# Delta rule in units of two heads: second unit's queries in the score banks, fifth unit's keys in the first chunk, a half's layer norm in the middle of the unit behind

## The chip, the cores and the metric

The kernel runs on one core of a Trainium2 chip. The metric is the device time of one execution in microseconds, the median over timed runs. The engines are PE (TensorE, with its weight loads as PEld), DVE (VectorE), ACT (ScalarE), POOL (GpSimd) and SP, which here only issues DMA transfers.

## The reference

Two transformer layers with post layer norm, on x of 2 batches x 1024 tokens x 256:

```python
def layernorm(x): m = mean(x); v = var(x); return (x - m) / sqrt(v + 1e-5)

x = layernorm(x + L0_attn(x))   # softmax attention, 32 query heads of 8, 8 key/value heads, rotary, causal
x = layernorm(x + L0_ffn(x))    # down(silu(x @ gate * s_gate) * (x @ up * s_up)) * s_down, int8 weights, 256 -> 1024 -> 256
x = layernorm(x + L1_attn(x))   # below
x = layernorm(x + L1_ffn(x))    # sign weights, relu, 256 -> 1024 -> 256

# L1_attn, 16 heads of 128
q, k, v = [silu(causal_depthwise_conv4(x @ W) + b) for W, b in (q, k, v)]
alpha, beta = sigmoid(x @ Wa + ba), sigmoid(x @ Wb + bb)
for t in range(T):              # S: 128 x 128 for each head
    err = S @ (k[t] * scale) - v[t]
    S = alpha[t] * S - beta[t] * outer(err, k[t] * scale)
    o[t] = S @ q[t]
o = (o - mean(o)) * rsqrt(var(o) + 1e-5) * ln_w + ln_b
return (o * sigmoid(x @ Wg)) @ Wo
```

## The kernel before

The kernel has three stretches. Up to about 679 us it does the first layer's attention and half of its int8 feed-forward. From there the second layer's attention begins beside the rest of the feed-forward, which ends with PE's last down product at 802.5 us. The delta rule proper fills the time to about 1950 us, and the second feed-forward runs in its last units and behind it.

The delta rule is worked in 32 **units**: a half of 512 tokens (there are four, `hi`) times a pair of heads (eight pairs, `s`; unit i is `hi, s = divmod(i, 8)`). A unit is four chunks of 128 tokens. `recur` goes through the chunks one after the other: `pr` (values turned, minus decayed keys times the state M), `prs` its copy on ACT, `pw` (times the inverse of the triangle `lt`), `wc` its copy, `pm` (the state's update, taken up by DVE into the next M, L697 or L699) and `po` (the outputs `o`).

Everything else of the neighbour units stands in between by **places**. A unit has 120 places. Each stream of work (`Places.add`) is a generator that yields the place at which it goes on; `Places.run` always takes the stream with the lowest place, and for the same place the one added first. From unit 0 on PE's order is exactly the order in which this emits the products (`te.strict`); the other engines' orders are made by the framework's scheduler, which simulates the program and prefers what was emitted earlier or marked `high_priority`. `after(a, b)` orders a behind b on their engine.

The parts that matter here:

- `project`, `conv`, `conv_out`: the queries, keys or values of a unit. Two banks (one for each head) take 6 products each; ACT scales a bank into `acc` (L268) and keeps its last three columns in `halos` (L272), DVE adds two taps of the convolution (L275), ACT makes the third (`far`, L289), POOL adds it (L292), ACT applies silu (L297). All projections take their banks from one pool of two, `ps_p` ("p"). The pool `ps_m` ("m", two banks) is for scores, turned keys, the gates and others.
- `keys`: the keys of unit i + 4 at place 91, then their triangle at 113 to 146: scans along the tokens (`at`, L325) and the products `pkk`.
- `rest_of_first`: emitted between the feed-forward's last block and unit 0. It loads the decays `dg` of unit 0, multiplies its keys and queries by them on POOL (L519, L521), then projects unit 1's values and queries, then unit 4's keys.
- `blocks` and `levels`: the triangle's inverse for two units, in chains of small DVE steps (L384, L390) and small products with copies (L420 to L479).
- `finish`: a unit's outputs, in the unit behind it, at places 41, 51, 101 and 111. The head outputs are normed (bias L595, scale on DVE, ACT and POOL, L602 and L605), turned (`pt`, L611), gated, split for precision (POOL, L618) and multiplied by Wo into `pf`; DVE adds that to the tokens `x` (L630). The pool of `x` (`xtok`) has one buffer, loaded for a half at its first unit's `finish`. At the half's last unit (`s == 7`) `finish` norms the tokens, two tiles after each `pf`, and stores them to `xs`, from where the second feed-forward takes them.
- `layernorm` (L919): for each tile of 128 tokens `bn_stats` and `bn_aggr`, then `rsqrt` over both tiles: three DVE steps (L905 to L907) and three rounds, either on DVE (three steps each, L910 to L912) or on POOL (four steps each, L914 to L917), then a DVE scaling for each tile (L926). The int8 feed-forward's blocks take POOL for the rounds; `finish` takes DVE.

The tokens `x` of the int8 feed-forward lie where the pools "late" and "w" are opened later, so the first tiles of these (`prs`, `dg`, `wg`) come after the last store of `x`.

The lists of places:

```python
UNIT, GAP = 120, 10
AT_ROWS, AT_QUERIES, AT_KC, AT_GATE, AT_GATE_ROWS, AT_SCORES = 1, 31, (42, 52), 61, 70.5, (71, 81)
AT_OUT = 9.5
AT_KEYS, AT_DECAY, AT_TRIANGLE = 91, 113, (131, 141, 146)
AT_LEVELS = 43, 53, 73, 83, 103, 113, 132, 142
AT_FINISH, AT_FINISH_LAST, AT_HALF = (41, 51, 101, 111), (31, 41, 71, 76), ((22, 30, 46), (12, 18, 36))
```

Of the kernel before, what the change touches and what calls it, by code (L numbers as in the profile page):

```python
# [31 lines left out]
HP = 2  # L32
# [56 lines left out]
AT_LEVELS = 43, 53, 73, 83, 103, 113, 132, 142  # L89
AT_FFN = 24  # L90
AT_FINISH, AT_FINISH_LAST, AT_HALF = (41, 51, 101, 111), (31, 41, 71, 76), ((22, 30, 46), (12, 18, 36))
# [53 lines left out]
def delta_rule(  # L145
# [39 lines left out]
    def bank(pool, tag, name):  # L185
        return pool.tile([P, HT], F32, name=name, tag=tag)
# [51 lines left out]

    def project(m, i, h):
        hi, s = place(i)  # L240
        if h == 0 and ("w" + m) not in st[i]:
            st[i]["w" + m] = weights(m, s)
        wh, wl = st[i]["w" + m]
        xh, xl = halves[hi]["xh"], halves[hi]["xl"]
        pp = bank(ps_p, "p", "pp")
        hs = slice(h * P, (h + 1) * P)
        for k in range(2):
            mm3(pp, wh[:, k, hs], wl[:, k, hs], xh[:, k, :], xl[:, k, :], k == 0, k == 1)
        return pp
# [10 lines left out]
    def conv(m, i, h, pp):  # L260
# [6 lines left out]
        with tc.high_priority():  # L267
            nc.scalar.activation(  # L268
                acc, pp, AF.Identity, bias=cb[:, n, hd : hd + 1], scale=cw[:, n, hd, KS - 1 : KS]
            )  # L270
            if hi % 2 == 0:
                nc.scalar.copy(halos[:, n, hd, :], pp[:, HT - KS + 1 :])  # L272

            for d in range(1, KS - 1):
                made = nc.vector.scalar_tensor_tensor(  # L275
                    acc[:, d:], pp[:, 0 : HT - d], cw[:, n, hd, KS - 1 - d : KS - d], acc[:, d:], ALU.mult, ALU.add
                )
                if m == "k" and d == 1 and solved:
                    after(made, solved[-1])
# [200 lines left out]

    def pair(m, i):

        pps = [project(m, i, h) for h in range(HP)]
        for h in range(HP):
# [73 lines left out]
    def rest_of_first():  # L558
# [4 lines left out]
        te.strict, te.last = True, ended[0]  # L563
        for m in "vq":
            drain(pair(m, 1))
        ks = keys(AHEAD, AT_KEYS)
        next(ks)
        lines.add(ks, next(ks), 0)

# [5 lines left out]
    def finish(i, o, m, chunks, places):  # L575

        hi, s = place(i)
        if s == 0:
            halves[hi]["x"] = load_tokens(pools["late"], hi * HC, HC)
        x = halves[hi]["x"]  # L580
        if chunks[0] == 0:
# [25 lines left out]
        for h in range(HP):  # L607
# [11 lines left out]
            sub_low(nc.gpsimd if i < last else nc.vector, yl, y, yh)  # L619
            ys.append((yh, yl))  # L620
        for c0 in range(0, nc_, 2):
            yield places[2 + c0 // 2]
# [7 lines left out]
            nc.vector.tensor_add(xc, pf, xc)  # L630
            if s == NS - 1:
                layernorm(gx, x, c1 + c0, 2)
                halves[hi]["done"] = c1 + c0 + 2
        if s == NS - 1 and hi < 2 * B - 1:
            store_tokens(xs, hi * HC, x)
# [183 lines left out]
    for i in range(-AHEAD, last + 1):  # L819
# [19 lines left out]
        elif 0 <= i < last:  # L839
            lines.add(others(i + 1), t + AT_ROWS, t)  # L840
        if i == 0:
            lines.add(gate_of_first(), t + AT_QUERIES)
        if i >= 0:
# [28 lines left out]
def tile_two_layers(ctx: ExitStack, tc: tile.TileContext, a, out):  # L872
# [45 lines left out]

    def layernorm(pool, x, t0, n, tag="ln", eng=None):  # L919
        m = pool.tile([P, n, 11], F32, name=tag, tag=tag)  # L920
        for i in range(n):
            nc.vector.bn_stats(m[:, i, 5:11], x[:, t0 + i, :])
            nc.vector.bn_aggr(m[:, i, 0:2], m[:, i, 5:11])
# [535 lines left out]
    def open_ffn(group):  # L1459
# [20 lines left out]
        def block(n):  # L1480
# [45 lines left out]
            with tc.high_priority() if n == NT - 2 else nullcontext():  # L1526
                for i in range(2):
                    y = new("fy", [P, E], 2)
                    nc.vector.tensor_mul(y, po[i], s_down)
                    nc.vector.tensor_add(x[:, n + i, :], y, x[:, n + i, :])  # L1530
                anchor["norm"] = layernorm(pool, x, n, 2, eng=nc.gpsimd)
                store_tokens(xs, n, x[:, n : n + 2, :])
# [129 lines left out]
```

## Time and profile before

| | us |
|---|---|
| timed runs | 2059.25, 2059.91, 2062.58 (median 2059.91) |
| the profiled execution | 2060.95 |
| its span in the trace | 2059.2 |
| mean granted PE clock | 0.979 |
| DVE, ACT, POOL busy | 1481.1, 1268.1, 1055.6 |
| last product of the int8 feed-forward | 802.5 |
| first `prs` copy of unit 0, of unit 1 | 819.8, 846.6 |
| end of the last layer norm of the int8 feed-forward; issue of its store | 814.7; 814.70 |
| issues of the stores of a finished half's tokens | 1148.4, 1742.0 (first and last of three) |

How to read it. One execution was taken; times count from its first instruction. PE's busy time is modelled from the start of each product, so a busy PE need not be at its peak. In a time line each row has a start, a length, the engine, the line, what is written and read, and in brackets how long the engine had been idle and which instruction released it. A wait for several things is put down to the one that came last. A granted clock of 1.00 is full speed; at 0.50 a product of 512 columns starts 0.43 us after the one before it instead of 0.23.

### The profile page before, as it was taken

Reading aid. Unit: us, or ns where it says so; the run is one execution under the profiler, and the core shown is the slowest. Engines: PE = TensorE matmul, PEld = TensorE weight load, DVE = VectorE, ACT = ScalarE, POOL = GpSimd, SP = SyncE. Lnnn points to the kernel's source line nnn. Section 1 sums busy time; section 2 is a strip of 40 time slices with the busy share of each in tenths; the row PEclk is TensorE's granted clock in tenths of the full one; section 3 lists DMA queues with packets and bytes.
Section 4 is the critical chain, followed back from the end, with each engine's and each line's share of the span. In section 5 each row is a group of like instructions: output and inputs, shape, how many; then the busy total and the mean of one; then the engine's idle time right before and its main releaser. Section 6 shows DMA issues by size and latency. Waiting matters only on the chain.

```text
span 2059.2 us, 49201 instructions
## 1 busy us (share of the span) xinstructions
PE 1891.8 (92%) x18657; PEld 1493.3 (73%) x18657; DVE 1481.1 (72%) x3557; ACT 1268.1 (62%) x2731; POOL 1055.6 (51%) x1635
## 2 busy tenths in 40 slices
PE   5898989999998898999999999998999999999886
PEld 3455555555556786889888888887888888888775
DVE  5756666877756886586778688678678678865676
ACT  1365566576755366567676676766677666686432
POOL 4353332331124565666776566666567676665430
PEclk8999999999999999999999999999999999999997
DMA  5554443442132432344444444444434434442010
GB/s 169 167 188 131 149 130 126 147 135 70 51 76 62 116 91 82 111 132 106 132 110 115 133 109 116 115 118 123 123 109 125 124 115 130 118 126 86 26 37 21
DMA packets 312997, 229.16 MB, mean 111 GB/s; under 512 B 139640, under 2 KB 278904, under 8 KB 312760
## 3 DMA queue, kind: packets, MB, share of 16 engines
q1 hardware_dynamic: 299640, 210.73, 35.1%
q10 hardware_dynamic: 9760, 10.83, 1.6%
q0 software_dynamic: 3360, 4.46, 0.9%
q8 instruction: 147, 2.41, 0.5%
q14 instruction: 90, 0.74, 0.1%
HBM read 171.18 MB, written 51.87 MB: 108 GB/s over the span
## 4 chain that ended last, share of the span: by engine, by line
PE 57%; DVE 13%; ACT 6%; DMA 5%; POOL 3%; issue 3%; SPq 1%; ACTq 0%; DVEq 0%; POOLq 0%
PE pp L942 5%; PE pp L944 4%; PE pp L943 4%; PE ps L1316 4%; PE av L1337 4%; PE ps L1247 3%; PE pkq L508 3%; PE pm L692 2%; DVE at L325 2%; PE pr L669 2%; PE pw L680 2%; PE po L708 2%; PE po L707 2%; PE p L478 2%; PE p L471 2%
## 5 line engine op out<-in xcount | busy, mean ns | idle before, releaser
L1256 DVE TENSOR_REDUCE mx<-ps 128x4 f32<-128x1024 f32 (+1 forms) x320 | 344.1, 1111 | 131.8 <-PE ps L1247 88.5
L1320 ACT ACTIVATE es<-ps 128x512 f32<-128x512 f32 (+1 forms) x608 | 314.2, 578 | 128.8 <-PE ps L1316 118.1
L1316 PE MATMUL ps<-qT,kT 128*128 128x512 f32 (+3 forms) x768 | 220.8, 371 | 19.4 <-ACT es L1320 18.6
L1247 PE MATMUL ps<-kT,qT 128*128 128x512 f32 x576 | 199.2, 420 | 26.8 <-DVE mx L1256 16.9
L1316 PEld LDWEIGHTS ps<-qT,kT 128*128 128x128 f32 x768 | 130.9, 190 | 106.4 <-ACT es L1320 59.6
L1247 PEld LDWEIGHTS ps<-kT,qT 128*128 128x128 f32 x576 | 101.6, 191 | 86.5 <-DVE mx L1256 45.8
L289 ACT ACTIVATE far<-pp,cw 128x509 f32<-128x509 f32 x192 | 133.4, 700 | 45.5 <-DVE k L275 18.6
L1337 PE MATMUL av<-es,vaug 128*32 128x512 f32 (+3 forms) x1536 | 157.7, 497 | 0.6 <-POOL es L1323 0.5
L1323 POOL TENSOR_SCALAR_AFFINE_SELECT es<-es 128x512 f32<-128x512 f32 x128 | 80.5, 638 | 147.0 <-ACT es L1320 144.0
L891 POOL TENSOR_TENSOR wfl<-wf,wfh 128x256 fp32r<-128x256 f32 x80 | 58.5, 735 | 185.7 <-ACT wfh L980 147.3
L275 DVE SCALAR_TENSOR_TENSOR q<-pp,cw,q 128x511 f32<-128x511 f32 (+1 forms) x128 | 93.3, 743 | 46.5 <-ACT halos L272 23.8
L275 DVE SCALAR_TENSOR_TENSOR k<-pp,cw,k 128x511 f32<-128x511 f32 (+1 forms) x128 | 92.1, 743 | 46.5 <-ACT k L268 25.3
L292 POOL TENSOR_TENSOR q<-q,far 128x509 f32<-128x509 f32 x64 | 69.5, 1088 | 95.0 <-ACT far L289 94.9
L275 DVE SCALAR_TENSOR_TENSOR v<-pp,cw,v 128x511 f32<-128x511 f32 (+1 forms) x128 | 92.2, 739 | 32.4 <-ACT v L268 18.2
L292 POOL TENSOR_TENSOR k<-k,far 128x509 f32<-128x509 f32 x64 | 77.8, 1217 | 52.0 <-ACT far L289 51.4
L519 POOL TENSOR_TENSOR k<-k,dg 128x508 f32<-128x508 f32 x64 | 82.2, 1284 | 33.7 <-PE pkq L508 29.8
L980 ACT CAST wfh<-wf 128x256 fp32r<-128x256 f32 x80 | 32.3, 405 | 105.9 <-DMA wf<-in_w1k 35.5
L708 PE MATMUL po<-wc,at 128*128 128x128 f32 x512 | 96.8, 276 | 0.0
L672 ACT COPY prs<-pr 128x256 f32<-128x256 f32 x128 | 48.9, 382 | 73.9 <-PE pr L669 65.8
L325 DVE TENSOR_TENSOR_SCAN at<-da,d 128x512 f32<-128x512 f32 x64 | 90.4, 1453 | 0.0
L680 PEld LDWEIGHTS pw<-prs,lt 128*128 128x128 f32 x512 | 76.7, 191 | 15.9 <-ACT prs L672 3.2
L692 PE MATMUL pm<-wc,kc 128*128 128x128 f32 x448 | 77.2, 295 | 11.8 <-ACT wc L683 11.7
(319 smaller groups left out, 5902.6 us busy)
## 6 DMA issues: line engine op xcount, KB each, us to landing
wk<-w1k SPq DMA_DIRECT2D x64, 256.0 KB
da<-dec SPq DMA_DIRECT2D x64, 256.0 KB
wv<-w1v SPq DMA_DIRECT2D x64, 256.0 KB
wq<-w1q SPq DMA_DIRECT2D x64, 256.0 KB
dg<-dec SPq DMA_DIRECT2D x64, 256.0 KB
wg<-w1g SPq DMA_DIRECT2D x64, 256.0 KB
wo<-w1o SPq DMA_DIRECT2D x64, 256.0 KB
ad<-avs ACTq DMA_DIRECT2D x32, 256.0 KB
```

The source lines that it names most:

```text
L275: made = nc.vector.scalar_tensor_tensor(acc[:, d:], pp[:, 0 : HT - d], cw[:, n, hd, KS - 1 - d : KS - d], acc[:, d:], ALU.mult, ALU.add)
L289: made = nc.scalar.activation(far[:, w], pp[:, w], AF.Copy, scale=cw[:, n, hd, 0:1])
L292: nc.gpsimd.tensor_add(acc[:, KS - 1 :], acc[:, KS - 1 :], far[:, w])
L325: nc.vector.tensor_tensor_scan(e, dec, d1.rearrange("p c t -> p (c t)"), 0.0, ALU.mult, ALU.add), taps
L680: te.link(nc.tensor.matmul(pw[:, r], lhsT=lt[:, h * HC + c, :], rhs=prs[:, r], start=True, stop=True))
L692: te.link(nc.tensor.matmul(pm[:, r], lhsT=st[i]["kc", h][:, c, :], rhs=wc[:, r], start=True, stop=True))
L708: te.link(nc.tensor.matmul(po[:, r], lhsT=st[i]["at", h][:, t], rhs=wc[:, r], start=(M is None), stop=True))
L1247: anchor["mm"] = te.link(nc.tensor.matmul(ps[:, j - j0, :].rearrange("p (g k) -> p g k", k=P), lhsT=q_, rhs=kT[:, :, j * P : (j + 1) * P], ...
L1256: nc.vector.tensor_reduce(mx[:, it, j0 // 2, :], ps[:, 0:n, :].rearrange("p j (g k) -> p g j k", k=P), AX.XY, ALU.max)
L1316: te.link(nc.tensor.matmul(ps[:, g - g0, :], lhsT=kT[:, g, jb * P : (jb + 1) * P], rhs=qT[:, i0 : i0 + w], start=True, stop=True,))
L1320: exps.append(nc.scalar.activation(es[:, g0 : g0 + n, 0:w], ps, AF.Exp, scale=D ** -0.5))
L1337: mm = te.link(nc.tensor.matmul(av[ROW * g : ROW * (g + 1), i0 - ih * 512 : 512], lhsT=vaugs[b][:, jb, kv, :], rhs=es[:, g, 0:w], start=(j ...
```

## The change

It has five parts.

1. `project` takes a pool as an argument, and `rest_of_first` gives the pool "m" to unit 1's queries. Values stay in "p".
2. Unit 1's value taps (`conv`, the first tap of `v` at `i == 1`) are ordered behind the last layer norm of the int8 feed-forward (`anchor["norm"]`). The rounds of that last block's `rsqrt` go to DVE; the other blocks keep POOL.
3. Unit 4's keys leave `rest_of_first`. They become a stream of unit 0, `first_keys`: projection and taps at place 1, the third tap and silu at 10.5, the rest at 113 and on as before.
4. A finished half's layer norm and store (all halves but the last) leave the places 101 and 111 of the unit behind its last unit and go to places 34 and 50 of the unit after that one (units 9, 17, 25), two tiles at each. The statistics are ordered behind the newest update of M that is emitted by then, and the `rsqrt` rounds run on POOL. The last half keeps its norm where it was.
5. The load of a half's tokens moves within `finish` from its start to just before place 101.

```diff
--- before.py
+++ after.py
@@ -87,7 +87,7 @@
 AT_KEYS, AT_DECAY, AT_TRIANGLE = 91, 113, (131, 141, 146)
 AT_BLOCKS, BLOCK_STEP = (44, 52, 145), 2.2
 AT_LEVELS = 43, 53, 73, 83, 103, 113, 132, 142
-AT_FFN = 24
+AT_FFN, AT_NORM = 24, (34, 50)
 AT_FINISH, AT_FINISH_LAST, AT_HALF = (41, 51, 101, 111), (31, 41, 71, 76), ((22, 30, 46), (12, 18, 36))
 
 FFN0, FFN1, FFN1_LAST, FFN1_TAIL = 7.6, 22.0, 27.0, 40.0
@@ -236,13 +236,13 @@
 
         return divmod(i, NS)
 
-    def project(m, i, h):
+    def project(m, i, h, psum=None):
         hi, s = place(i)
         if h == 0 and ("w" + m) not in st[i]:
             st[i]["w" + m] = weights(m, s)
         wh, wl = st[i]["w" + m]
         xh, xl = halves[hi]["xh"], halves[hi]["xl"]
-        pp = bank(ps_p, "p", "pp")
+        pp = bank(*(psum or (ps_p, "p")), "pp")
         hs = slice(h * P, (h + 1) * P)
         for k in range(2):
             mm3(pp, wh[:, k, hs], wl[:, k, hs], xh[:, k, :], xl[:, k, :], k == 0, k == 1)
@@ -275,6 +275,8 @@
                 made = nc.vector.scalar_tensor_tensor(
                     acc[:, d:], pp[:, 0 : HT - d], cw[:, n, hd, KS - 1 - d : KS - d], acc[:, d:], ALU.mult, ALU.add
                 )
+                if m == "v" and i == 1 and d == 1:
+                    after(made, anchor["norm"])
                 if m == "k" and d == 1 and solved:
                     after(made, solved[-1])
         return made
@@ -478,9 +480,9 @@
                     te.link(nc.tensor.matmul(p4[A, u, :], lhsT=n3[Z, u, :], rhs=lt[Z, u, Z], start=True, stop=True))
             nc.scalar.copy(st[i + n]["lt"][A, :, Z], p4[A])
 
-    def pair(m, i):
-
-        pps = [project(m, i, h) for h in range(HP)]
+    def pair(m, i, psum=None):
+
+        pps = [project(m, i, h, psum) for h in range(HP)]
         for h in range(HP):
             conv(m, i, h, pps[h])
         if i < last:
@@ -561,11 +563,16 @@
             for h in range(HP):
                 decayed(0, h, which)
         te.strict, te.last = True, ended[0]
-        for m in "vq":
-            drain(pair(m, 1))
+        for m, psum in (("v", (ps_p, "p")), ("q", (ps_m, "m"))):
+            drain(pair(m, 1, psum))
+
+    def first_keys():
+
         ks = keys(AHEAD, AT_KEYS)
         next(ks)
-        lines.add(ks, next(ks), 0)
+        yield AT_ROWS + AT_OUT
+        yield next(ks)
+        yield from ks
 
     def gate_of_first():
         gate(0)
@@ -575,9 +582,6 @@
     def finish(i, o, m, chunks, places):
 
         hi, s = place(i)
-        if s == 0:
-            halves[hi]["x"] = load_tokens(pools["late"], hi * HC, HC)
-        x = halves[hi]["x"]
         if chunks[0] == 0:
             st[i]["wo"] = []
             for part in range(2):
@@ -618,6 +622,9 @@
             (nc.gpsimd.tensor_copy if i < last else nc.scalar.copy)(yh, y)
             sub_low(nc.gpsimd if i < last else nc.vector, yl, y, yh)
             ys.append((yh, yl))
+        if s == 0:
+            halves[hi]["x"] = load_tokens(pools["late"], hi * HC, HC)
+        x = halves[hi]["x"]
         for c0 in range(0, nc_, 2):
             yield places[2 + c0 // 2]
             pf = bank(pools["t"], "t", "pf").rearrange("p (c e) -> p c e", e=E)
@@ -628,10 +635,15 @@
                     mm3(pf[:, c, :], yh[:, t], yl[:, t], wo[0][:, h, :], wo[1][:, h, :], h == 0, h == HP - 1)
             xc = x[:, c1 + c0 : c1 + c0 + 2, :]
             nc.vector.tensor_add(xc, pf, xc)
-            if s == NS - 1:
+            if s == NS - 1 and i == last:
                 layernorm(gx, x, c1 + c0, 2)
                 halves[hi]["done"] = c1 + c0 + 2
-        if s == NS - 1 and hi < 2 * B - 1:
+        if s == NS - 1 and i < last:
+
+            for n in range(0, HC, 2):
+                yield UNIT + AT_NORM[n // 2]
+                made = updated[-1]
+                layernorm(gx, x, n, 2, eng=nc.gpsimd, behind=made)
             store_tokens(xs, hi * HC, x)
 
     def recur(i):
@@ -839,6 +851,7 @@
         elif 0 <= i < last:
             lines.add(others(i + 1), t + AT_ROWS, t)
         if i == 0:
+            lines.add(first_keys(), t + AT_ROWS, t)
             lines.add(gate_of_first(), t + AT_QUERIES)
         if i >= 0:
             lines.add(recur(i), t, chain=True)
@@ -916,10 +929,12 @@
                 eng.tensor_scalar(t, t, -0.5, 1.5, ALU.mult, ALU.add)
                 eng.tensor_mul(y, y, t)
 
-    def layernorm(pool, x, t0, n, tag="ln", eng=None):
+    def layernorm(pool, x, t0, n, tag="ln", eng=None, behind=None):
         m = pool.tile([P, n, 11], F32, name=tag, tag=tag)
         for i in range(n):
-            nc.vector.bn_stats(m[:, i, 5:11], x[:, t0 + i, :])
+            made = nc.vector.bn_stats(m[:, i, 5:11], x[:, t0 + i, :])
+            if behind:
+                after(made, behind)
             nc.vector.bn_aggr(m[:, i, 0:2], m[:, i, 5:11])
         rsqrt(m[:, :, 2], m[:, :, 1], m[:, :, 3], m[:, :, 4], eng=eng)
         for i in range(n):
@@ -1528,7 +1543,7 @@
                     y = new("fy", [P, E], 2)
                     nc.vector.tensor_mul(y, po[i], s_down)
                     nc.vector.tensor_add(x[:, n + i, :], y, x[:, n + i, :])
-                anchor["norm"] = layernorm(pool, x, n, 2, eng=nc.gpsimd)
+                anchor["norm"] = layernorm(pool, x, n, 2, eng=nc.gpsimd if n < NT - 2 else None)
                 store_tokens(xs, n, x[:, n : n + 2, :])
             yield 0.2
```

## The prediction

> **What bounds it now.** I read the page's busy table first, then the matrix engine's idle stretches, then the units one by one, then the queues behind the two worst places. The profiled execution took 2060.95 us, of which the trace spans 2059.2 us. The median of the three timed runs, 2059.91 us, is 1.04 us lower.
>
> ```profile
> PE 1891.8 (92%) x18657; PEld 1493.3 (73%) x18657; DVE 1481.1 (72%) x3557; ACT 1268.1 (62%) x2731; POOL 1055.6 (51%) x1635
> ```
>
> PE is busy 92% of the span, so what can be won lies in the 167 us in which PE waits, and in the stretches where its clock is halved. I took the start of a unit from its first `prs` copy on ACT (L672) and asked for the busy time between such starts. Columns: length, then busy us of PE, PEld, DVE, ACT, POOL, granted clock, DMA share, GB/s. These are units 7, 9, 15, 17, 23 and 25, and last the seam from the last product of the int8 feed-forward to the start of unit 1:
>
> ```profile
> 1055.50:1095.30 39.80, 37.92 (x654) 33.61 (x653) 29.38 (x76) 28.15 (x60) 28.66 (x48) 1.00 0.40 115
> 1128.90:1172.40 43.50, 37.88 (x646) 33.67 (x645) 32.08 (x104) 27.49 (x61) 25.19 (x41) 0.96 0.43 128
> 1351.30:1390.50 39.20, 37.05 (x650) 33.06 (x650) 26.81 (x62) 27.09 (x65) 26.76 (x41) 1.00 0.40 113
> 1421.30:1471.20 49.90, 40.11 (x651) 34.77 (x651) 35.43 (x105) 28.94 (x67) 27.00 (x41) 0.90 0.39 114
> 1649.00:1688.80 39.80, 37.75 (x654) 33.62 (x653) 29.42 (x76) 28.02 (x60) 28.62 (x48) 1.00 0.40 116
> 1722.40:1761.90 39.50, 36.58 (x648) 32.50 (x647) 32.08 (x104) 27.30 (x60) 25.68 (x42) 1.00 0.46 142
> 802.50:846.60 44.10, 33.71 (x170) 27.30 (x169) 27.11 (x79) 20.84 (x50) 22.24 (x31) 0.85 0.49 152
> ```
>
> Units 9, 17 and 25 have about 28 more DVE instructions than 7 and 23: the layer norm of a finished half falls at their start. It costs 10.1 us in unit 17 (49.9 against 39.8), 3.7 us in unit 9 and nothing in unit 25. How, the time lines of PE and DVE in unit 17 show (start, length, engine, instruction, idle time before it and its releaser):
>
> ```profile
> 1441.06 1.07 PE L611 MATMUL pt<-ident,o 128*128 128x128 f32 x3 [7.11 <-POOL o L605]
> ...
> 1439.99 0.79 DVE L926 TENSOR_SCALAR xtok<-xtok,ln 128x256 f32<-128x256 f32 x2
> 1440.70 0.16 DVE L595 SCALAR_TENSOR_TENSOR om<-om 128x8 f32<-128x8 f32 x1
> ```
>
> L595 makes the bias for the head outputs. It stands in DVE's queue behind the last rows of the norm, so `o` is scaled late and PE's transposes L611 wait 7.11 us; PE runs the next 5 us (1441 to 1446) at a granted clock of 0.50. The seam, on PE and DVE:
>
> ```profile
> 807.29 0.50 PE L942 MATMUL pp<-x2h,wq 128*128 128x512 f32 x1 [1.81 <-ACT far L289]
> 813.41 0.50 PE L942 MATMUL pp<-x2h,wk 128*128 128x512 f32 x1 [1.51 <-ACT far L289]
> 816.59 0.49 PE L942 MATMUL pp<-x2h,wk 128*128 128x512 f32 x1 [1.51 <-ACT far L289]
> 820.24 0.68 PE L680 MATMUL pw<-prs,lt 128*128 128x128 f32 x4 [1.77 <-issue]
> 826.03 0.77 PE L669 MATMUL pr<-M,k 128*128 128x128 f32 x2 [1.81 <-DVE M L697]
> ...
> 813.62 1.04 DVE L926 TENSOR_SCALAR x<-x,ln 128x256 f32<-128x256 f32 x1
> 814.67 0.73 DVE L275 SCALAR_TENSOR_TENSOR q<-pp,cw,q 128x510 f32<-128x510 f32 x1
> ```
>
> Each projection waits until ACT's `far` has read the bank it wants; the last layer norm ends at 814.66, and its store, the `dg` and `wg` loads and the first tile of the late pool queue behind it. PE does 33.7 us of work in 44.1 us, 10 of them at half clock (821.6 to 831.9).
>
> **The seam, step by step.** Unit 1's values stay at 802.5 to 805.5. Its queries now take the two `m` banks, last read at 797.2 by L1042, so they follow at once: 12 products at 0.235 us, to 808.3. The norm reaches its aggregates at 804.9 as before. Then, instead of 12 POOL steps among `v` adds (808.36 to 812.60), DVE does 12 dependent steps 0.20 us apart (the pace of the last norm in the program, 2031.07 to 2033.07): 2.4 us, and two scalings, 0.7 us, so 808.0, or 809.5 if two query taps of 0.75 us get between. I take 808.5 in place of 814.66. New wait: the value taps (4 x 0.75 us) stand behind it, 808.5 to 811.5; behind them in DVE's queue are the query taps and the solve of units 2 and 3, and who waits is ACT's `far`, so the `p` banks. The first bank is free at 810.9 (tap, 0.2, `far` 0.69), the second at 812.4. Unit 4's keys, now after unit 0's first transposes, are 6 products each, 811.0 to 812.4 and 812.5 to 813.9; PE loses 2.3 us ahead of them. The store goes out at 808.6 (wq's two loads, 811.70 and 812.15 before, stand ahead of it on SP and wait for the same queries, 808.3), lands 2.1 us later (814.70 to 816.84), so `prs` is ready at 811. `pw` follows the keys at 814.0, for 820.24.
>
> The next wait is `pr` of the second chunk (826.03), which needs M and the decayed keys. M: `pm` would end at 816, M at 816.5; with the two scans of unit 4 ahead of it in DVE's queue, as now (821.36 to 825.58), up to 3 us more. Decayed keys: the first L519 started at 819.87, 4.7 us after the first `dg` issue at 815.16; that issue moves to 809.1, so 813.8, then three POOL products at 1.27 us, and one or two of the six 1.09 us adds between: 818.7. I take 818.7: 7.3 us earlier. Of the half clock after 821.6 (some 6 us of work in 825 to 832, 3 us at full clock) I count 1 us back, since a gap of 2.3 us stays. Seam: -8.3. Bounds: -2, if the queries' and keys' ACT and POOL work, now crowded into a shorter stretch, leaves only the 1.8 and 1.5 us waits; -12, if M is not behind the scans and all the clock comes back. The moved keys bring nothing new: 12 products, 4 taps, 8 ACT instructions, 2 POOL adds and two `wk` loads for unit 5, out of the stretch before unit 0 into it, under unit 0's own waits.
>
> The Trainium skill speaks against the last microsecond: TensorE: Matmul & The Clock Gate, section "What's actually happening", has the clock drop after an idle window of about 3.4 us. The trace has a clock of 0.51 in 825 to 832 though no idle stretch of the seam is over 1.81 us. By the page the clock gives 0 here and the seam -7.3.
>
> **The half's norm.** It leaves the start of units 9, 17, 25 for their places 34 and 50 of 120, behind the first chunk's M. Gone: 10.1 us in unit 17; in unit 9 1.3 us surely (the level product L431 waits 2.26 us there and 0.7 to 1.2 elsewhere), 3.7 at most, since 1.65 us of its idle time is put down to issue: 2.5; in unit 25 0. New: per unit 4 statistics (0.41), 4 aggregates (0.17), 6 small steps (0.16) and 4 scalings (0.41), 4.9 us of DVE, less 18 steps (2.9 us) that leave it; and 24 POOL steps 0.28 us apart, 6.7 us. Cover: DVE has 10.4 us and POOL 11.1 us idle in unit 7. Without it, a chain of 12 POOL steps (3.4 us) lies ahead of POOL's copies L439, for which the next level products wait. So 0 to 3.4 a unit; 1 each, nearer the cover. The half's tokens are stored about as early (1148.4 now), and the next half's load, moved behind place 51, still stands 13 us ahead of its use at place 101; what it holds up on SP (`wg`, `dg`) is held up now by the same pair (1148.40, 1152.07). Cost 0; 2 if the norm slides past the middle. Sum: -10.1 - 2.5 + 3 = -9.6; bounds -13.8 and -1.2.
>
> A rule against this part: GPSIMD Engine Reference, "Engine selection", gives VectorE for elementwise work and GpSimd as about half as fast. The rows have 0.28 us a step on POOL against 0.20 on DVE; an estimate by the page's factor is 0.40, 9.6 us of POOL for 6.7, still under its 11.1 us idle.
>
> **Sum.** 2060.95 - 8.3 - 9.6 = 2043.0 in the profiled execution, 2042 as a median (-1.04).
>
> **Rivals.** (1) Only the norm's part arrives: the value taps, held behind the norm, and POOL's crowd eat the seam to -2: 2059.9 - 11.6 = 2048. For: ACT's `far` releases three of five PE waits, and it moves from 806.55 to 810. Against: the store is 6 us earlier whatever the taps do. 0.14. (2) Only the seam arrives, the norm costing in the middle what it cost at the start: 2051.6. For: DVE is 72% busy. Against: nothing like L595 waits at place 34. 0.10. (3) Slower: POOL. In each of the three units DVE's scalings wait for POOL's chain, with the M update behind them, and PE stalls as in unit 17, 10.1 us: 3 x 10.1 - 13.8 (old norms) - 8.3 = +8.2: 2068. It decides from 7.4 us a unit, (13.8 + 8.3) / 3. For: POOL is dense between the level products. Against: 11 idle us. 0.09. (4) The change does its parts, but the orders of DVE and POOL, made anew all along, give it back (unit 11 and 19 differ by such from 43.6 to 44.4, the gates' units): 2058 to 2062. 0.07.
>
> **From cases to numbers.** My forecast, 0.60: 2042, its own range 2034 to 2049. The range 2031 to 2056 takes in rivals 1 and 2 and the bounds (2060 - 26 and -3). What a measurement tells from no change is about 0.2%, 4 us. Forecast and rivals 1, 2 are faster: 0.84; rival 4 the same: 0.07; rival 3 slower: 0.09.
>
> **What would show it.** Queries following values on PE without a gap; the norm's end near 808.5 and the store behind it; `pr` of chunk 2 near 819; units 9, 17 and 25 all near 40 to 41 us; no wait of L611 over 2 us in unit 17. Wrong: a norm past 812, scans ahead of M, or new waits for POOL's L917 or L439 in the three units.

## The result, and the profile after

The changed kernel takes **2080.02 us** (median of five executions, 2079.33 to 2086.73), the kernel before 2059.91 (2059.25 to 2063.86) beside it: a ratio of 1.0093, 95% interval 1.0076 to 1.0110. The forecast was 2042, its range 2031 to 2056: the sign is wrong. The profiled execution is the one of 2086.73 us, with a span of 2085.0, 25.8 longer than that of before. By stretches (seam: from the last product of the int8 feed-forward to the first `prs` copy of unit 1):

| stretch | before, us | after, us | difference |
|---|---|---|---|
| up to the seam | 802.7 | 808.1 | +5.4 |
| seam | 43.9 | 45.8 | +1.9 |
| units 1 to 8 | 282.3 | 283.3 | +1.0 |
| unit 9 | 43.5 | 53.6 | +10.1 |
| units 10 to 16 | 248.9 | 249.3 | +0.4 |
| unit 17 | 49.9 | 44.9 | -5.0 |
| units 18 to 24 | 251.2 | 250.2 | -1.0 |
| unit 25 | 39.5 | 54.0 | +14.5 |
| unit 26 to the end | 297.3 | 295.8 | -1.5 |

The first row isn't the change's: up to there both kernels run the same instructions in the same order on every engine, and in the fourteen profiled executions of this study the seam begins anywhere from 797.9 to 811.1 us. So single executions are compared below by stretches, and kernels by medians.

The busy table of the page after, and the windows of units 9, 17, 25 and the seam (length, busy us of PE, PEld, DVE, ACT, POOL, granted clock, DMA share, GB/s):

```profile
PE 1900.1 (91%) x18657; PEld 1500.5 (72%) x18657; DVE 1476.5 (71%) x3512; ACT 1269.0 (61%) x2731; POOL 1064.8 (51%) x1695
```

```profile
1137.20:1190.80 53.60, 38.33 (x645) 34.48 (x644) 31.89 (x90) 28.61 (x63) 34.60 (x78) 0.86 0.41 125
1440.10:1485.00 44.90, 40.53 (x652) 35.91 (x651) 32.48 (x87) 28.24 (x67) 30.54 (x65) 0.92 0.44 126
1735.20:1789.20 54.00, 37.02 (x645) 33.07 (x644) 32.81 (x90) 28.61 (x63) 35.78 (x80) 0.87 0.36 110
808.06:853.90 45.84, 33.75 (x168) 28.25 (x168) 26.48 (x88) 20.67 (x50) 19.71 (x19) 0.78 0.49 146
```

PE does the same work in the seam (33.7 us), and about the same in units 9 and 25, but stands there for 15 and 17 us. The engines' shares say nothing of it: POOL has 35 us of work in a unit of 54. The time line of unit 9 names the chain (PE, then POOL, DVE and SP's queue):

```profile
1184.42 0.58 PE L957 MATMUL pf<-wo,yh 128*128 128x256 f32 x1 [12.40 <-DVE xtok L637]
...
1150.45 0.35 POOL L927 TENSOR_TENSOR ln<-ln 128x2 f32<-128x2 f32 x2 [2.75 <-DVE ln L920]
...
1160.72 0.20 POOL L927 TENSOR_TENSOR ln<-ln 128x2 f32<-128x2 f32 x1
1160.87 1.27 POOL L521 TENSOR_TENSOR k<-k,dg 128x508 f32<-128x508 f32 x1
...
1164.54 1.29 POOL L523 TENSOR_TENSOR q<-q,dg 128x512 f32<-128x512 f32 x1
1165.78 0.20 POOL L927 TENSOR_TENSOR ln<-ln 128x2 f32<-128x2 f32 x1
...
1168.50 0.11 POOL L316 MEMSET lt<- 128x8 f32 x1 [2.37 <-PE pw L692]
1170.21 1.08 POOL L294 TENSOR_TENSOR k<-k,far 128x509 f32<-128x509 f32 x1 [1.60 <-ACT far L291]
1171.26 1.11 POOL L928 TENSOR_TENSOR ln<-ln 128x2 f32<-128x2 f32 x1
1172.34 1.15 POOL L929 TENSOR_SCALAR ln<-ln 128x2 f32<-128x2 f32 x1
...
1175.67 0.20 POOL L930 TENSOR_TENSOR ln<-ln 128x2 f32<-128x2 f32 x1
...
1170.71 2.78 DVE L327 TENSOR_TENSOR_SCAN at<-da,d 128x512 f32<-128x512 f32 x2
...
1175.32 1.38 DVE L941 TENSOR_SCALAR xtok<-xtok,ln 128x256 f32<-128x256 f32 x4
1183.68 0.69 DVE L637 TENSOR_TENSOR xtok<-pf,xtok 128x512 f32<-128x512 f32 x1 [3.21 <-DMA xtok<-xs]
...
1176.73 0.37 SPq L914 DMA_DIRECT2D xs<-xtok  x1
1179.85 0.36 SPq L910 DMA_DIRECT2D xtok<-xs  x1
```

Read it from the end. PE waits for the residual add L637, which empties a bank for the next half of the output product. The add waits for the next half's tokens. Their load L910 goes out only when the store L914 of the finished half has left the one buffer of `xtok`, and the store waits for the scalings L941. These wait for POOL: the 24 small steps of the two pairs begin at 1150.45 and end at 1175.87, with four decayed products, casts, far adds, copies and two long waits between them. Counted from each row's start to the next row's (or to its own end, if that comes first), these 25.4 us hold 5.7 us of the norm's own steps, 14.9 of other work, and 4.8 of standing.

In unit 17 the same 24 steps come in another order of POOL's queue and take 9.5 us from first to last; the chain ends in time, and no transpose L615 waits over 0.8 us: the forecast's gain there came, as 5.0 us instead of 10.1.

The seam after (PE, ACT, POOL):

```profile
820.95 0.79 PE L957 MATMUL pp<-x2h,wk 128*128 128x512 f32 x1 [5.68 <-ACT far L291]
830.82 1.22 PE L704 MATMUL pm<-wc,kc 128*128 128x128 f32 x4 [4.67 <-ACT wc L695]
...
820.21 1.26 ACT L291 ACTIVATE far<-pp,cw 128x509 f32<-128x509 f32 x2 [0.45 <-DVE v L275]
828.56 0.69 ACT L291 ACTIVATE far<-pp,cw 128x509 f32<-128x509 f32 x1 [3.82 <-POOL v L294]
830.37 0.39 ACT L695 COPY wc<-pw 128x256 f32<-128x256 f32 x1
...
822.51 1.27 POOL L521 TENSOR_TENSOR k<-k,dg 128x508 f32<-128x508 f32 x1 [15.16 <-DVE tmp L386]
827.44 2.13 POOL L294 TENSOR_TENSOR v<-v,far 128x509 f32<-128x509 f32 x2
```

Five short waits have become two long ones. Unit 4's keys want the values' banks, which wait for the held taps (820.2). And POOL's queue has the four decayed products, which wait for `dg` (issued at 817.21) until 822.51, ahead of the values' far adds. The row's bracket names DVE's L386, but that writes nothing the products read. The two buffers of `far` stay taken until those adds, so ACT can't make the third `far` before 828.56, nor `wc` behind it before 830.37.

### The profile page after: what moved, and what is told of

Read it like the earlier page. It is cut to its first block, busy times and chain, and to the rows that moved or that the text cites. A ratio compares the mean times of both kernels' runs of the same rounds, so it can differ in the third digit from the quotient of the medians.

```text
span 2085.0 us, 49215 instructions
## 1 busy us (share of the span) xinstructions
PE 1900.1 (91%) x18657; PEld 1500.5 (72%) x18657; DVE 1476.5 (71%) x3512; ACT 1269.0 (61%) x2731; POOL 1064.8 (51%) x1695
## 4 chain that ended last, share of the span: by engine, by line
PE 58%; DVE 11%; ACT 7%; DMA 6%; POOL 3%; issue 2%; SPq 1%; ACTq 0%; DVEq 0%; POOLq 0%
PE pp L957 5%; PE pp L959 4%; PE pp L958 4%; PE ps L1331 4%; PE av L1352 4%; PE ps L1262 3%; PE pkq L510 3%; PE pm L704 2%; PE po L720 2%; DVE at L327 2%; PE pr L681 2%; PE pw L692 2%; PE po L719 2%; PE p L480 2%; PE pkk L340 2%
## 5 line engine op out<-in xcount | busy, mean ns | idle before, releaser
L275 DVE SCALAR_TENSOR_TENSOR v<-pp,cw,v 128x510 f32<-128x510 f32 (+1 forms) x128 | 92.1, 740 | 39.6 <-ACT v L268 25.5
L957 PE MATMUL pf<-wo,yh 128*128 128x256 f32 x256 | 78.8, 308 | 30.9 <-DVE xtok L637 30.7
L294 POOL TENSOR_TENSOR k<-k,far 128x509 f32<-128x509 f32 x64 | 78.1, 1222 | 48.4 <-ACT far L291 47.8
L684 ACT COPY prs<-pr 128x256 f32<-128x256 f32 x128 | 48.9, 382 | 75.5 <-PE pr L681 63.8
L704 PE MATMUL pm<-wc,kc 128*128 128x128 f32 x448 | 77.6, 296 | 16.1 <-ACT wc L695 16.0
L294 POOL TENSOR_TENSOR v<-v,far 128x509 f32<-128x509 f32 x64 | 69.1, 1086 | 38.7 <-ACT far L291 38.7
```

The costliest lines, as they stand in the source:

```text
L275: made = nc.vector.scalar_tensor_tensor(acc[:, d:], pp[:, 0 : HT - d], cw[:, n, hd, KS - 1 - d : KS - d], acc[:, d:], ALU.mult, ALU.add)
L294: nc.gpsimd.tensor_add(acc[:, KS - 1 :], acc[:, KS - 1 :], far[:, w])
L704: te.link(nc.tensor.matmul(pm[:, r], lhsT=st[i]["kc", h][:, c, :], rhs=wc[:, r], start=True, stop=True))
L957: te.link(nc.tensor.matmul(out, lhsT=lhi, rhs=rhi, start=k0, stop=False))
```

## The experiments

Two theories. **A**: the loss is in units 9 and 25, because the norm's steps on POOL are stretched by the work between them and the next half's residual comes late. **B**: it comes from the seam and what its new order shifts. Units and seams below are from each kernel's profiled execution; ratios are to the kernel before on the same chip, with 95% intervals.

**The norm's part alone, the seam's part alone.** First the seam undone:

```diff
-        for m, psum in (("v", (ps_p, "p")), ("q", (ps_m, "m"))):
-            drain(pair(m, 1, psum))
+        for m in "vq":
+            drain(pair(m, 1))
+        first_keys()
...
-                if m == "v" and i == 1 and d == 1:
-                    after(made, anchor["norm"])
...
-                anchor["norm"] = layernorm(pool, x, n, 2, eng=nc.gpsimd if n < NT - 2 else None)
+                anchor["norm"] = layernorm(pool, x, n, 2, eng=nc.gpsimd)
```

> Only the held-back norm and the moved load are left of the change; unit 1's queries, unit 5's keys, the hold on the value taps and the engine of the seam's last norm are as before. Theory A (the loss is the next half's residual: the norm's 24 small steps stand in POOL's queue between other work, so scalings, store, load and the residual add end late, and PE stands 12.4 and 13.5 us in units 9 and 25; unit 17 wins 5.1): 2078 us (2074 to 2083), units 9 and 25 near 54, unit 17 near 45, the seam 44 as before. Theory B (the loss comes from the seam, whose new order of POOL and DVE shifts all that follows): 2060 to 2066.

Measured: 2084.68 us, ratio 1.0124 (1.0105 to 1.0143); seam 44.4, units 9, 17, 25 at 52.7, 50.4 and 54.5. Unit 17 stalls as well here, which A had not foreseen, so the time lies 2 us above A's range:

```profile
1477.14 0.55 PE L953 MATMUL pf<-wo,yh 128*128 128x256 f32 x1 [9.63 <-DVE xtok L634]
```

Then the norm and the load put back:

```diff
-            if s == NS - 1 and i == last:
+            if s == NS - 1:
                 layernorm(gx, x, c1 + c0, 2)
                 halves[hi]["done"] = c1 + c0 + 2
-        if s == NS - 1 and i < last:
-
-            for n in range(0, HC, 2):
-                yield UNIT + AT_NORM[n // 2]
-                made = updated[-1]
-                layernorm(gx, x, n, 2, eng=nc.gpsimd, behind=made)
+        if s == NS - 1 and hi < 2 * B - 1:
             store_tokens(xs, hi * HC, x)
```

> Only the seam's part is left of the change; norm and load of a half are as before. Theory A: 2062 us (2059 to 2065), the seam from the int8 feed-forward's last product to unit 1 at 45 to 46 us, units 9, 17 and 25 at 43.5, 50 and 39.5 as before. Theory B: 2074 to 2080. My forecast's seam (-8.3) would be 2052, and is taken as refuted by the trace of the changed kernel.

Measured: 2057.73 us, ratio 0.9985 (0.9973 to 0.9997); seam 45.1; units 40.0, 49.7, 39.8. The time lies 1 us under A's range, far from B's: the whole loss is the norm's part. Unit 9 is 40.0 with the norm at its old place, where the profile of before had 43.5, so the 3.7 us that unit 9 had over unit 7 don't come with the old norm in every kernel.

**The norm's rounds on DVE.**

```diff
-                layernorm(gx, x, n, 2, eng=nc.gpsimd, behind=made)
+                layernorm(gx, x, n, 2, behind=made)
```

> The change as it is, but the held-back norm's nine or so rounds run on DVE (18 steps of 0.2 us for the two pairs) instead of 24 on POOL. Theory A: the scalings end 6 to 10 us earlier, the stalls before the second half of the output product in units 9 and 25 shrink from 12.4 and 13.5 to 0 to 5 us: 2057 us (2052 to 2066). Rival (the trip by store and load, 6.5 us, or DVE's order, not POOL's queue, sets it): 2074 or more.

Measured: 2049.73 us, ratio 0.9944 (0.9927 to 0.9961): one argument is worth 30 us against the change, and the kernel is now faster than before, 2 us below A's range. Unit 9 on DVE (time line), and units 9, 17, 25 (windows, columns as above):

```profile
1132.57 1.36 DVE L935 BATCH_NORM_STATS2 ln<-xtok 128x6 f32<-128x256 f32 x4
...
1145.82 1.38 DVE L941 TENSOR_SCALAR xtok<-xtok,ln 128x256 f32<-128x256 f32 x4
...
1159.83 0.68 DVE L637 TENSOR_TENSOR xtok<-pf,xtok 128x512 f32<-128x512 f32 x1
```

```profile
1126.20:1165.40 39.20, 35.60 (x646) 31.93 (x645) 31.83 (x104) 27.52 (x60) 24.92 (x41) 1.00 0.47 139
1413.30:1457.80 44.50, 40.32 (x651) 35.84 (x651) 34.63 (x105) 28.20 (x66) 26.56 (x41) 0.92 0.45 129
1707.90:1747.70 39.80, 35.89 (x648) 32.25 (x647) 32.29 (x104) 27.78 (x60) 25.67 (x42) 1.00 0.46 139
```

From the first statistics to the end of the last scaling it takes 14.6 us, DVE doesn't stand ahead of the residual add, and no wait of PE in the unit is over 1.5 us. This row gives the deadline too. From the last scaling's end to the add the changed kernel needs 7.0 us (1176.70 to 1183.68). So here the last scaling could end as late as 1152.8, 20.3 us after the first statistics. With POOL it took 33.2: 12.9 too late, and PE stood 12.4.

**The DVE rounds without the seam's part.** The edits of the first and the third kernel together:

> Only the held-back norm and the moved load, with the norm's rounds on DVE; the whole seam is as before. Theory A (the seam's part is worth nothing or +1 to +2; the norm's part alone is worth what units 9 and 17 show, 4 and 5 us): 2050 us (2047 to 2053), unit 9 near 39.5, unit 17 near 44.5, unit 25 near 39.5, seam 44. Rival (the seam's part is what made the version with DVE rounds fast): 2056 to 2060.

Measured: 2053.24 us, ratio 0.9958 (0.9941 to 0.9975), just above A's range of 2047 to 2053; seam 45.0, units 39.2, 46.9, 39.6 (the profiled execution is the slowest of eleven, 2060.00 us). The held-back norm is a gain by itself once its rounds are on DVE. The 3.5 us between this and the kernel with the changed seam aren't settled: the intervals overlap, and single executions here go from 2043.65 to 2060.00.

**What on POOL stretches the chain.** The keys' taps put behind the scalings, so that the keys' far adds can't stand ahead of the norm's last steps:

```diff
-                layernorm(gx, x, n, 2, eng=nc.gpsimd, behind=made)
+                anchor["half"] = layernorm(gx, x, n, 2, eng=nc.gpsimd, behind=made)
...
+                if m == "k" and d == 1 and "half" in anchor:
+                    after(made, anchor["half"])
```

> The change as it is, the norm's 24 small steps still on POOL, but the following keys' first taps are put behind the norm's scalings on DVE, so that the keys' memset, far adds and the rest of that work can't stand ahead of the norm's steps on POOL. Theory A (it is the order in POOL's queue that makes the norm end 32 us after it began; without it the 24 steps need 7 to 15 us): stalls ahead of the second half of the output product at 0 to 5 us, 2056 to 2068. Rival (24 POOL steps among other work need the 32 us whatever stands ahead; or the taps, held, stop the bank of the projections): 2076 to 2090.

Measured: 2078.03 us, ratio 1.0073 (1.0054 to 1.0092). The chain takes 27.4 us in unit 9 for 33.2, the stand there is 7.66 us for 12.40; units 47.8, 48.9, 49.9. By the deadline of 20.3 it should stand 7.1. So A's 0 to 5 us missed, and the time lies in the rival's range (2076 to 2090), though the rival's 32 us aren't there either. The keys' work is 6 us of the stretch, and what remains stands among the steps, the memset for the keys' triangle and its wait included (time line of POOL; its line numbers are two higher):

```profile
1162.48 0.19 POOL L929 TENSOR_TENSOR ln<-ln 128x2 f32<-128x2 f32 x1
1162.63 1.27 POOL L523 TENSOR_TENSOR k<-k,dg 128x508 f32<-128x508 f32 x1
...
1167.78 0.20 POOL L929 TENSOR_TENSOR ln<-ln 128x2 f32<-128x2 f32 x1
...
1170.50 0.11 POOL L318 MEMSET lt<- 128x8 f32 x1 [2.37 <-PE pw L694]
```

By these rows no single block is to blame: 7.1 us were missing, and the largest block left, the four decayed products, takes about 5. Each pair's 12 steps depend on one another, so what stands between two of them adds to the chain. No run moved the other blocks one by one.

**Fewer steps.** One round in place of three, so 8 steps a unit in place of 24; the kernel leaves out the other two:

```diff
-        for _ in range(3):
+        for _ in range(rounds):
...
-        rsqrt(m[:, :, 2], m[:, :, 1], m[:, :, 3], m[:, :, 4], eng=eng)
+        rsqrt(m[:, :, 2], m[:, :, 1], m[:, :, 3], m[:, :, 4], eng=eng, rounds=1 if behind else 3)
```

> The change as it is, but the held-back norms leave out two of the three rounds of their inverse square root (8 POOL steps in a unit and not 24; the output is less exact). Theory A: the scalings come ahead of the key taps in DVE's queue and end 10 us earlier or more, and the 12.4 and 13.5 us stalls go: 2052 to 2060. Rival (the trip by store and load, 7 us from the last scaling to the residual add, is too long in any case): 2068 to 2076.

Measured: 2046.78 us, ratio 0.9928 (0.9912 to 0.9945), 33 us under the change, below A's range; units 39.0, 39.4, 42.8, the chain 13.9 us. So with 8 steps POOL does no harm; it is the number of dependent steps that have to find their way through a full queue. The trip by store and load, the rival, is not too long in itself.

**An earlier place.**

```diff
-AT_FFN, AT_NORM = 24, (34, 50)
+AT_FFN, AT_NORM = 24, (14, 28)
```

> The change as it is, the norm's rounds on POOL, but its two places are 20 and 22 earlier (14 and 28 of 120 in place of 34 and 50). Theory A (POOL's queue, with other work between the steps, stretches the chain; the last pair's last step still stands behind the keys' work in POOL's queue): the first statistics come 4 to 7 us earlier, the last scaling hardly so; stalls of 8 to 13 us stay in units 9 and 25: 2070 to 2080. Rival (only the place is too late): 2052 to 2066.

Measured: 2074.68 us, ratio 1.0066 (1.0045 to 1.0087), in A's range; units 52.1, 45.7, 49.4. In unit 9 the first statistics come 6.7 us earlier from the unit's start (-0.3 for +6.4), the last scaling 4.0 us (35.6 for 39.6), and PE stands 11.20 us for 12.40:

```profile
1131.17 0.73 DVE L935 BATCH_NORM_STATS2 ln<-xtok 128x6 f32<-128x256 f32 x2
...
1141.17 1.57 DVE L941 TENSOR_SCALAR xtok<-xtok,ln 128x256 f32<-128x256 f32 x2
1166.34 0.71 DVE L941 TENSOR_SCALAR xtok<-xtok,ln 128x256 f32<-128x256 f32 x2
1176.52 0.69 DVE L637 TENSOR_TENSOR xtok<-pf,xtok 128x512 f32<-128x512 f32 x1 [1.64 <-DMA xtok<-xs]
```

The first pair is done 11.6 us after its statistics; the second ends 29.1 us after its own (they begin at 1137.94), in the crowd of the unit's middle. POOL's last step there ends at 1162.82; the last scaling then stands on DVE behind the keys' taps and a scan, and from its end to the add it takes 9.5 us, for 7.0 in the change. The place alone isn't the cause.

**The seam: values' far adds first on POOL.** The four decayed products of unit 0 are emitted behind unit 1's projections and ordered behind the values' last far add:

```diff
-        for which in "kq":
-            for h in range(HP):
-                decayed(0, h, which)
         te.strict, te.last = True, ended[0]
         for m, psum in (("v", (ps_p, "p")), ("q", (ps_m, "m"))):
             drain(pair(m, 1, psum))
+        for which in "kq":
+            for h in range(HP):
+                decayed(0, h, which)
...
+            if m == "v" and i == 1:
+                anchor["v"] = made
...
+            if i == 0:
+                after(made, anchor["v"])
```

> The change as it is, but in the seam the four decayed products of unit 0 stand behind the two far adds of unit 1's values in POOL's queue, not ahead of them (a wait for dg no longer holds the adds). Theory A (POOL's 15 us of standing before 822.5 hold the far adds, these hold ACT's two far buffers, and ACT's wc stands behind them): third far 5 us earlier, seam 45.9 to 41 to 43: 2076 us (2074 to 2078). Rival (the far rows wait for the taps anyway): no change, 2080; or, with the decayed keys late for the second chunk, up to 3 more.

Measured: 2086.34 us, ratio 1.0122 (1.0103 to 1.0142). The seam is 40.8, as A said; the time misses A's 2074 to 2078 by 8 us, above all since unit 17 stalls at 50.6, for 44.9 in the change, with the chain at 27.6 us there. The time lines of PE and POOL in the seam (line numbers up to six higher):

```profile
818.24 0.80 PE L963 MATMUL pp<-x2h,wk 128*128 128x512 f32 x1 [5.69 <-ACT far L291]
824.08 0.71 PE L710 MATMUL pm<-wc,kc 128*128 128x128 f32 x4 [0.75 <-ACT wc L701]
...
818.27 2.13 POOL L294 TENSOR_TENSOR v<-v,far 128x509 f32<-128x509 f32 x2 [13.59 <-ACT far L291]
820.36 2.52 POOL L523 TENSOR_TENSOR k<-k,dg 128x508 f32<-128x508 f32 x2
```

The 4.67 us ahead of `pm` have become 0.75; the 5.7 ahead of the keys are untouched.

**Both cures together**, the values first and the DVE rounds:

> Both cures together: the held-back norm's rounds on DVE, and in the seam the values' far adds ahead of the decayed products on POOL. Theory A: the two add up; the seam is 40 to 42 us (40.8 with the values first, 44.2 with the norm on DVE alone), units 9, 17 and 25 stay at 39, 44.5 and 40: 2046 us (2043 to 2049). Rival (the seam's gain is given back in a later unit, since the queues' orders are made anew, as unit 17 gave 5.8 us back when only the values came first): 2050 or more.

Measured: 2046.94 us, ratio 0.9931 (0.9917 to 0.9945); seam 40.9, units 39.2, 45.2, 39.9. That lies in A's range. With POOL's queue free of the norm, units 9, 17 and 25 give only 0.8 us of the seam's gain back; the times alone don't show that gain, since the interval overlaps that of the DVE rounds without it (0.9927 to 0.9961). This version is faster than the kernels before and after the change, and leaves nothing out of the computation.

**What holds the keys' banks.** To both cures, the query taps too are held behind the seam's last norm:

```diff
-                if m == "v" and i == 1 and d == 1:
+                if m in "vq" and i == 1 and d == 1:
```

> As with both cures (norm's rounds on DVE, values' far adds ahead of the decayed products), and the query taps too are held behind the seam's last norm, so that its last step no longer stands behind a query tap (it waited 2 us there). Theory A (the norm ends 2.5 to 3 us earlier, and the taps, banks and keys behind it): seam 38 to 39.5 for 40.9, 2044.5 us (2042 to 2047). Rival (the keys' banks, not the norm, set the seam): no change, 2047.

Measured: 2047.59 us, ratio 0.9923 (0.9901 to 0.9945); seam 41.2. The norm does end early (5.3 us after the last product, forecast 5.8), and it changes nothing, as the rival said. DVE's time line tells why:

```profile
802.48 0.74 DVE L947 TENSOR_SCALAR x<-x,ln 128x256 f32<-128x256 f32 x2
...
804.19 0.75 DVE L275 SCALAR_TENSOR_TENSOR q<-pp,cw,q 128x511 f32<-128x511 f32 x1 [0.89 <-ACT halos L272]
804.86 1.40 DVE L275 SCALAR_TENSOR_TENSOR v<-pp,cw,v 128x511 f32<-128x511 f32 x2
...
806.25 1.40 DVE L275 SCALAR_TENSOR_TENSOR q<-pp,cw,q 128x511 f32<-128x511 f32 x2
807.56 1.40 DVE L275 SCALAR_TENSOR_TENSOR v<-pp,cw,v 128x510 f32<-128x510 f32 x2
```

Between the norm's end (803.2) and the values' last tap (ended 809.0) stand three query taps and a wait; the banks come free only then, and the keys start at 810.08 after 5.18 us.

**The hold moved from the values to the queries, and no hold at all**, both with the DVE rounds and without the edit of the decayed products:

```diff
-                if m == "v" and i == 1 and d == 1:
+                if m == "q" and i == 1 and d == 1:
```

> The held-back norms' rounds on DVE; in the seam the hold is taken from the value taps and put on the query taps, so DVE's order is values, norm, queries, and the values' far adds come ahead of the decayed products on POOL by themselves. Theory A (PE's 5.7 us stand ahead of unit 4's keys because the value taps, and so ACT's far and the banks, wait for the norm; the decayed products must not hold the values' far adds): that stand shrinks to 1 to 3 us, the norm ends some 3 us later than with the hold, the seam is 38 to 41 us, 2045 us (2041 to 2048). Rival (the keys' stand only moves on to the second chunk, which waits for the decayed keys, later with the norm): seam 43 to 46, 2048 to 2053.

Measured: 2050.66 us, ratio 0.9952 (0.9931 to 0.9973); seam 43.8. On POOL the values' far adds now come ahead of the decayed products by themselves (the adds 5.6 and 8.1 us after the last product, the products from 15.9), so it was the hold on the values that had put the products first. The keys no longer wait (no idle time over 0.5 us ahead of them), but `pw` waits 4.13 us for `prs`, which comes after the norm's store, and the gates' projections 2.19. The time and the seam are in the rival's ranges.

```profile
817.80 1.23 PE L692 MATMUL pw<-prs,lt 128*128 128x128 f32 x4 [4.13 <-ACT prs L684]
```

```diff
-                if m == "v" and i == 1 and d == 1:
-                    after(made, anchor["norm"])
```

> The held-back norms' rounds on DVE; in the seam no tap is held behind the norm. The norm's steps then stand between the taps of values, queries and keys in DVE's queue, and its end comes some 6 us later. Theory A (the hold is needed for the norm's end, which dg and the decayed keys wait for): seam 44 to 49 us, 2049 to 2055. Rival (the hold itself is the loss): seam 39 to 42, 2044 to 2048.

Measured: 2050.68 us, ratio 0.9950 (0.9931 to 0.9969); seam 45.8, nearly all its idle time in one place, ahead of `pw`:

```profile
821.82 1.22 PE L690 MATMUL pw<-prs,lt 128*128 128x128 f32 x4 [10.98 <-ACT prs L682]
```

Time and seam lie in A's ranges, and the norm does end late, 16.1 us after the last product, for 7.3 to 8.8 in the six kernels that have the change's seam as it is. But the seams of these six go from 44.2 to 45.9, and the interval overlaps that of the DVE rounds with the hold (0.9927 to 0.9961). So the rival is refuted, and that the hold is needed isn't shown. Values and norm compete for DVE behind the same product; whichever goes first, PE waits for the other.

## Why the prediction was wrong

**The step that failed** is the cost of the half's norm at its new place: "New: per unit ... 24 POOL steps 0.28 us apart, 6.7 us. Cover: DVE has 10.4 us and POOL 11.1 us idle in unit 7 ... So 0 to 3.4 a unit; 1 each", and with it "the next half's load ... still stands 13 us ahead of its use ... Cost 0; 2 if the norm slides past the middle". The steps' own time was near (5.7 us against 6.7). What was taken for their price was busy time set against idle time, for a chain of dependent steps in a queue with work between them. In its place the runs show an elapsed time against a deadline: 33.2 us from first statistics to last scaling where 20.3 were to be had, 12.4 us of PE standing, and 14.4 us more in unit 9 than with the rounds on DVE (53.6 against 39.2). For the three units the term was to be +3; measured against the kernel with DVE rounds it is 14.4 + 0.4 + 14.2 = +29.0, and the medians say 30.3.

**The gain of the old norms** was forecast as 10.1 + 2.5 + 0. With the rounds on DVE, and against the kernel with the old norm and the changed seam, it is 49.7 - 44.5 = 5.2 in unit 17, 0.8 in unit 9, 0 in unit 25. The wait of L611 did go. In its place unit 17 waits 2.42 us for DVE's L425, which now has the norm's rounds ahead of it. Unit 9's 2.5 was read from a unit of one kernel's order that another kernel with the same norm doesn't repeat.

**The next half's load** was seen and priced at nothing. Its chain through one buffer (store, load, add: 7.0 us) turns a late norm into a wait of PE. The 13 us ahead of its use held only while the norm ended on time.

**The seam**, forecast -8.3 with bounds -2 and -12, is +1.9 in the profile, outside its bounds. Queries did follow values without a gap. The norm's end 5.8 us after the last product was 8.7 in the change, since its last step stood behind a query tap, and 5.3 with the query taps held. Two terms failed. The first bank was to be free 8.2 us after the last product, behind the values' taps ("808.5 to 811.5 (4 x 0.75 us)"), with 2.3 us lost by PE; the keys start 12.9 us after it and wait 5.7. 2.9 us of that are the norm's late end (1.5 to 3.0 in the six kernels with this seam); with the norm early, the query taps that then stand among the value taps keep the wait at 5.2. And POOL's order was put as adds between the decayed products, by the order of before; under the hold the scheduler puts all four products ahead of the values' adds. That is worth 5 us: 45.8 against 40.8. So `pr` of the second chunk, forecast 16.2 us after the last product, came at 26.0 (23.4 before, 20.1 with the values first). With it mended the seam is 40.8 to 41.2, against 43.9 to 45.0 in the three kernels that have it as before: a gain of some 3.4 us, inside the forecast's bounds but less than half of its 8.3.

**The rivals.** The third, at 0.09, had the sign and half the mechanism: DVE's scalings waiting for POOL's chain, 10.1 us of stall a unit. It put the update of M behind them, and that wasn't held up; the victim was the next half's tokens. "Against: 11 idle us" is the same mistake as in the sum. The forecast's range was 1 us narrower at the top than its own bounds (2060 - 3 is 2057, not 2056), which doesn't matter here. The rule on GpSimd's speed that was weighed beside the sum changed nothing: the steps' own time, 5.7 us, lay under both of its figures, 6.7 and 9.6.

**The clock**, one microsecond of the seam: the granted clock of the seam was 0.85 before, 0.78 after, and 0.89 with both cures, with the long wait ahead of the keys still there. Its share of the seam's gain isn't separated from the waits.

Open: why unit 17 escapes in one order of POOL's queue (17.7 us) and not in another (27.3 and 27.6). The orders differ between kernels whose code for that unit is the same, so it is the scheduler's choice; no run set it alone, and none gave the norm's steps precedence in POOL's queue. A second buffer for the tokens, which would take the store out of the trip, wasn't tried.

## What to carry to other kernels

A chain of small dependent steps on an engine with a long in-order queue is priced by what stands between its steps, not by its own busy time or the engine's idle share: count the work ahead of each step, and compare the elapsed time with the last moment at which the result is needed. When a step is moved, follow it through its buffer to the next user (here store, load, add) and work out that deadline first. An order constraint on one engine moves other engines' queues too, since the scheduler places the rest around it.

## What the runs showed of the hardware

A small POOL step of 128 x 2 takes 0.20 us, but 1.11 and 1.15 us at 1171.26 and 1172.34 in the fence of unit 9 above, while DVE ran two scans (L327, 1170.71 to 1173.49). The other way round, DVE's L918 took 0.80 us for 0.17 to 0.20 beside a far add on POOL. The Trainium skill, SBUF — State Buffer, section "SBUF: two separate sides", has the port pair of the two engines as an exclusive lock: for a DVE instruction in a two-port mode, or with two SBUF inputs beside a POOL instruction that reads SBUF, the one that comes second blocks for the whole of the other's instruction. The scans' row agrees: they read two tiles, and the second slow step ends when they end, at 1173.49. Whether L918 falls under that condition no run shows, and none separated the two engines.

After a stand PE pays once more. The windows behind the stands of units 9 and 25 in the changed kernel:

```profile
1184.40:1187.60 3.20, 3.17 (x15) 2.95 (x16) 0.21 (x1) 0.00 (x0) 0.00 (x0) 0.50 0.00 0
1187.60:1190.80 3.20, 3.20 (x23) 3.08 (x22) 0.49 (x1) 0.62 (x2) 0.00 (x0) 0.50 0.52 169
1190.80:1194.00 3.20, 3.20 (x10) 2.48 (x10) 0.00 (x0) 1.01 (x2) 0.00 (x0) 0.61 0.00 0
...
1784.30:1787.50 3.20, 3.17 (x17) 2.95 (x18) 0.21 (x1) 0.00 (x0) 0.00 (x0) 0.54 0.01 3
1787.50:1790.00 2.50, 2.50 (x26) 2.25 (x24) 0.48 (x1) 0.95 (x2) 0.00 (x0) 1.00 0.63 209
```

An estimate from these clocks: the 6.4 us of PE's work at 0.50 behind the first stand would be 3.2 at full clock, and the 3.2 us at 0.61 would be 2.0, so a stand of 12.4 costs up to 4.4 us beyond itself. Unit 9, which ends at 1190.8, is 14.4 us longer than with the rounds on DVE, 2.0 more than the stand. Behind the second stand the clock is back within about 3.2 us.
